# A decoder layer on one core: small TensorE pieces moved to other places of a hand-written order

## The chip, the core and the metric

The kernel runs on one core of a Trainium2 chip. The time is the device time of one execution in microseconds, median of three runs: 906.37 us (906.29 to 906.52). Less is better. All data are float32. TensorE's granted clock in the profile is 0.998 of full speed over the span, so that times of one row can be compared with those of another.

## The reference, cut to what matters

x has 4096 rows (16 batches of 256) of 256 channels. Three stages, each followed by a layer norm:

```python
# 1: four heads of 64 channels against fixed keys k and values v (256 of them)
q = layernorm(x, ln_g, ln_b)
a = x + square(relu(q_h @ k.T)) @ v              # per head h
h = layernorm(x + a)
# 2: 16 heads of 16 channels, 256 queries by 256 keys per batch
attn = gamma * (Q K^T) / 4 + delta * (ap * max(D, 0) + an * min(D, 0))   # D: clipped differences
h = layernorm(h + softmax(attn) @ V @ Wo.T + bo)
# 3: a feed-forward net with one of 8 experts per row
e = argmax(h @ gate_W.T + gate_b)
f = relu(h @ wi.T + wi_b + (h @ A_e.T) @ B_e.T) @ wo.T + wo_b
out = layernorm(h + f)
```

## The kernel before, in words

The order of all work is written out by hand (`tc.manual_schedule()`, L905 on). Engines run side by side, each works through its own queue in that order, and an instruction waits only for semaphores.

**Stage one** takes eight blocks of 512 rows. A block has eight steps m, two channel halves c by four pairs of n. In a step TensorE computes two score tiles in 64x64 tiles (L311, sixteen matmul records in all), ScalarE takes the relu (L319), VectorE the square (L321), and one step later TensorE multiplies with the values (L331, sixteen records). So TensorE's queue reads: scores of step m, values of step m-1, then whatever the list `steps[m]` holds. Such pieces are: turning the normalised rows of the next block into columns (`turn_in`, L292), turning the sums of the last block back (`turn_out`, L354, two halves of four 128x128 transposes) with VectorE's addition (L360, `y`), statistics (L185, L186), the scale (`scaling`, L202 to L240) and the norm of the last block's rows into `hid` (`norm_out`, L245 on ScalarE, then L376 on GpSimd).

PSUM has eight banks. In stage one two of them are the pool psB (`tile_b`), which the pieces use in turn: a third `tile_b` waits until the first has been read. From the end of stage one on (`turns.append(0)`) `tile_b` goes round three banks.

`biases()` (L140 to L172) folds two biases into others, in four parts: spreading bv, its product with Wo (L147), turning `bo` (L154, copied by VectorE into `columns`, L156), and the product with Wq (L161, subtracted by VectorE, L169). The parts stood at steps 2 to 5 of block 1.

During the last block the first pieces of stage two are made: `turned` (L421, rows of batch 0 into columns), `keys` (L460, whose rows SyncE's queue then scatters into kM) and `queries` (L434), at steps 4, 5 and 6. The first block starts by turning its rows (L292), with ScalarE's and VectorE's evictions to `xnT` (L296, L301), after 30 idle transposes (L910).

**Stage two** is a loop over 64 groups n, four heads of one batch each. Group n: scores (`logits`, L612, in 32-row tiles, into four banks that ScalarE has filled with the positive part of the bias, `positive`, L603), attention product of group n-2 (`attend`, L668, 32-column tiles), row maxima on VectorE (L627, which also adds the negative part that GpSimd prepared, `negative`, L591), turns of the score tiles of group n-1 (`turned`, L652, two tiles, then later two more) with the exponential on ScalarE (`exps`, L659), and the subtraction of the maxima (L642, half on GpSimd and half on VectorE). Between the two pairs of turns stands a large piece (queries L434, keys L460, values L482 or the output product L564 of another batch), if there is one; in group 5 there was none. `keep` copies the attention sums out (L681), the values are copied by L490.

**The feed-forward net** of six blocks is spread over groups 15 to 62, eight groups (parts 0 to 7) for each: rows normalised in part 7 of the block before (`rows`, four L245 on ScalarE), turned in part 0 (`turn`, L752, L755), gates in part 1 (`gates`, L767, 64-column tiles, then ScalarE's copy `gT`), routing and the inner products (L838, L850) in parts 2 and 3, the outer product (L868) in parts 4 to 7. Blocks six and seven of the net follow the loop.

The last stage-one block's sums (`rest`, block 7) were turned in group 0 into `y`, measured in groups 16 to 19 and normalised into `hid` in groups 27, 28, 29 and 35 (`LATE`). Block 6 was finished within stage one.

## Time and profile before

| | us |
|---|---|
| median of three runs | 906.37 |
| the profiled execution's own time | 906.51 |
| its span | 904.72 |
| stage one, 0 to 257: TensorE / VectorE / ScalarE / GpSimd busy | 253.49 / 215.56 / 184.64 / 60.97 |
| groups 0 to 14, 257 to 347 | 86.85 / 81.40 / 73.74 / 81.94 |
| groups with the net, 347 to 830 | 481.98 / 377.74 / 302.96 / 244.48 |
| end, 830 to 904.7 | 69.35 / 32.48 / 10.69 / 2.77 |

The 1.79 us between the span and the profiled execution's time lie around the span. A line of the timeline reads: start, duration, engine and source line, operation, out<-in, active rows and columns of TensorE's array, shape, number of records, and in brackets the idle time before it with what ended it. Matmuls are pipelined: one starts before the one ahead of it has ended, so the time that a run of them takes is read from its start to the next start. PE is TensorE, PEld its weight loads, DVE VectorE, ACT ScalarE, POOL GpSimd.

### The profile page before, as it was taken

How to read it: one execution, taken by the hardware profiler on the slowest of the kernel's cores; microseconds unless marked ns; L12 is line 12 of the kernel's file. 1: busy time of each engine (PE TensorE's matmuls, PEld its weight loads, DVE VectorE, ACT ScalarE, POOL GpSimd, SP SyncE). 2: the span in 40 equal slices, each digit the busy share in tenths (PEclk: the TensorE clock that was granted, in tenths of full speed). 3: DMA queues.
4: the chain of work that ended last, by engine and by line, in shares of the span. 5: the costliest groups of instructions: out<-in, count | busy, mean ns of one | idle time of the engine just before them, and what ended most of it. 6: DMA issues, size and time to landing. Idle time of an engine off the chain costs nothing.

```text
span 904.7 us, 19055 instructions
## 1 busy us (share of the span) xinstructions
PE 891.7 (99%) x6940; PEld 548.0 (61%) x6940; DVE 707.2 (78%) x1980; ACT 572.0 (63%) x953; POOL 390.2 (43%) x381
## 2 busy tenths in 40 slices
PE   8999999999999999999999999999999999999997
PEld 4333333333356776578658757865875786587555
DVE  5888898989878998878777887877788788678444
ACT  5767787778688878466556846655674575566111
POOL 1102312231469997534634653573465347344010
PEclk9999999999999999999999999999999999999999
DMA  5411011100001222010111102011110201111101
GB/s 139 147 36 36 31 39 39 65 2 1 4 10 50 71 72 57 13 42 18 39 43 41 50 14 66 17 39 42 41 51 12 68 18 39 41 28 43 24 0 47
DMA packets 44190, 37.01 MB, mean 41 GB/s; under 512 B 14912, under 2 KB 40000, under 8 KB 44096
## 3 DMA queue, kind: packets, MB, share of 16 engines
q1 hardware_dynamic: 43520, 35.52, 14.1%
q8 instruction: 55, 0.90, 0.4%
q14 instruction: 39, 0.32, 0.1%
q10 hardware_dynamic: 576, 0.26, 0.1%
HBM read 21.07 MB, written 6.03 MB: 30 GB/s over the span
## 4 chain that ended last, share of the span: by engine, by line
PE 59%; DVE 1%; ACT 1%; issue 0%; DVEq 0%; ACTq 0%
PE ps_l L838 12%; PE ps_b L652 10%; PE ps_b L868 7%; PE ps_l L612 5%; PE ps_v L668 5%; PE ps_v L868 5%; PE ps_b L564 3%; PE ps_b L482 2%; PE ps_b L434 2%; PE ps_b L460 2%; PE ps_l L850 2%; PE ps_b L767 1%; PE ps_b L752 1%; PE ps_b L421 1%; PE ps_b L838 0%; PE ps_b L812 0%
## 5 line engine op out<-in xcount | busy, mean ns | idle before, releaser
L591 POOL TENSOR_SCALAR neg<-dneg,aneg,delta 128x512 f32<-128x512 f32 x217 | 187.4, 876 | 207.3 <-PE ps_b L652 129.1
L627 DVE CUSTOM_DVE_ANT_0 neg<-ps_l,neg 128x256 f32<-128x256 f32 x512 | 181.6, 420 | 30.1 <-PE ps_l L612 25.6
L603 ACT ACTIVATE ps_l<-dpos,apos_d 128x512 f32<-128x512 f32 x256 | 173.4, 687 | 40.8 <-DVE mx L627 37.5
L321 DVE TENSOR_TENSOR pr<-r 128x1024 f32<-128x1024 f32 x128 | 155.4, 1254 | 31.3 <-ACT r L319 31.0
L659 ACT ACTIVATE pT<-ps_b 128x512 f32<-128x512 f32 x256 | 142.7, 590 | 56.6 <-PE ps_b L652 54.5
L319 ACT ACTIVATE r<-ps_a 128x1024 f32<-128x1024 f32 x128 | 126.5, 1022 | 57.4 <-PE ps_a L311 31.8
L652 PE MATMUL ps_b<-ident,neg 128*128 128x128 f32 x1024 | 139.1, 278 | 2.8 <-ACT pT L659 2.6
L652 PEld LDWEIGHTS ps_b<-ident,neg 128*128 128x128 f32 x1024 | 113.0, 140 | 38.8 <-issue 16.2
L642 POOL TENSOR_TENSOR neg<-neg,mx 128x1024 f32<-128x1024 f32 x65 | 123.8, 1906 | 21.2 <-DVE mx L627 20.2
L331 PE MATMUL ps_v<-pr,vv 64*64 64x512 f32 x1024 | 123.5, 593 | 0.3
L311 PE MATMUL ps_a<-xnT,kT 64*64 64x512 f32 x1024 | 122.2, 592 | 0.7 <-ACT xnT L296 0.4
L838 PE MATMUL ps_l<-xt,wi 128*128 128x512 f32 x248 | 111.5, 595 | 0.0
L642 DVE TENSOR_TENSOR neg<-neg,mx 128x1024 f32<-128x1024 f32 x63 | 92.3, 1465 | 0.3
L346 POOL TENSOR_TENSOR xt<-xt,half 128x512 f32<-128x512 f32 x15 | 23.8, 1585 | 138.4 <-ACT half L345 138.4
L331 PEld LDWEIGHTS ps_v<-pr,vv 64*64 64x64 f32 x1024 | 38.1, 132 | 70.7 <-issue 43.2
L311 PEld LDWEIGHTS ps_a<-xnT,kT 64*64 64x64 f32 x1024 | 37.6, 133 | 67.0 <-issue 55.5
L612 PE MATMUL ps_l<-kM,qT 32*128 32x256 f32 x1024 | 74.8, 401 | 0.4 <-ACT ps_l L603 0.4
L838 PEld LDWEIGHTS ps_l<-xt,wi 128*128 128x128 f32 x248 | 45.3, 190 | 49.0 <-issue 44.6
L868 PE MATMUL ps_b<-wof,hT 128*128 128x256 f32 x304 | 68.4, 380 | 0.0
L668 PE MATMUL ps_v<-pT,vaug 128*32 128x256 f32 x1024 | 67.5, 384 | 0.8 <-ACT pT L659 0.8
L861 DVE TENSOR_SCALAR hT<-ps_l,wib 128x512 f32<-128x512 f32 x43 | 29.8, 746 | 44.0 <-PE ps_l L850 44.0
L868 PEld LDWEIGHTS ps_b<-wof,hT 128*128 128x128 f32 x304 | 57.5, 190 | 9.2 <-issue 1.5
(119 smaller groups left out, 1055.7 us busy)
## 6 DMA issues: line engine op xcount, KB each, us to landing
cT<-in_ctxT SPq DMA_DIRECT2D x16, 256.0 KB
kM<-keys SPq DMA_DIRECT2D x128, 32.0 KB
v<-raw SPq DMA_DIRECT2D x128, 32.0 KB
invs<-rows SPq DMA_DIRECT2D x128, 32.0 KB
x<-in_x SPq DMA_DIRECT2D x7, 512.0 KB
out<-x SPq DMA_DIRECT2D x7, 512.0 KB
frow<-in_frac SPq DMA_DIRECT2D x16, 128.0 KB
wi<-in_wiT SPq DMA_DIRECT2D x1, 1024.0 KB
```

The costliest lines, as they stand in the source:

```text
L311: nc.tensor.matmul(sc[64 * k : 64 * k + 64, h, :], lhsT=kT[64 * h : 64 * h + 64, q, hf * P + 64 * k : hf * P + 64 * k + 64], rhs=self.xnT[ ...
L319: nc.scalar.activation(r, sc, AF.Relu)
L321: nc.vector.tensor_tensor(pr, r, r, ALU.mult)
L331: nc.tensor.matmul(self.acc[k][64 * h : 64 * h + 64, :], lhsT=vv[64 * k : 64 * k + 64, hf, 64 * q : 64 * q + 64], rhs=pr[64 * k : 64 * k + ...
L591: nc.gpsimd.tensor_scalar(self.neg[:, g], self.batch.dneg, aneg[:, h : h + 1], delta, ALU.mult, ALU.mult,)
L603: nc.scalar.activation(banks[g], self.batch.dpos.rearrange("p j k -> p (j k)"), AF.Copy, scale=apos_d[:, h : h + 1],)
L627: nc.vector.tensor_tensor_reduce(out=self.t[:, g, j, :], in0=banks[g][:, j * S : (j + 1) * S], in1=self.neg[:, g, j, :], scale=1.0, scalar ...
L642: eng.tensor_tensor(rows, rows, top.to_broadcast([P, 4, S]), ALU.subtract)
L652: nc.tensor.transpose(ps[:, k * S + j * P : k * S + (j + 1) * P], self.t[:, g, j, k * P : (k + 1) * P], ident,)
L659: nc.scalar.activation(self.pT[:, g, :], self.ps[g], AF.Exp)
L838: nc.tensor.matmul(self.banks[g], lhsT=wi[:, c, f * P : (f + 1) * P], rhs=self.xT[:, c, :], start=(c == 0), stop=False,)
L868: nc.tensor.matmul(ps[:, 0:C], lhsT=self.hT[f][:, j * P : (j + 1) * P], rhs=wof[:, f, :], start=(f == 0), stop=(f == FC - 1),)
```

## The change

Eight edits, none of which adds or removes a matmul:

- The first block's rows are turned by a new `turn_first`: the first channel half goes into two PSUM tiles, ScalarE evicts 256 columns from one and VectorE 256 from the other; the second half goes through a bank of the pool psV.
- The last two parts of `biases()` move from steps 4 and 5 of block 1 to step 1 of blocks 2 and 3, directly ahead of that step's two half turns.
- Block 6 isn't finished within stage one: its sums are turned in group 5 as the large piece (`turn_both`), written into `hid` instead of `y`.
- Blocks 6 and 7 are measured in groups 16 to 21, 27 and 28, scaled together in group 29 and normalised in groups 35 to 37 and 43 (block 6) and 44, 45, 51, 52 (block 7), in place.
- `turned` and `keys` of batch 0 stand together at step 4 of the last block.
- `queries` of batch 0 stands at its step 7, ahead of the last values, and VectorE evicts it instead of ScalarE.
- `gates` stands directly behind `attend` in part 1, instead of behind the large piece; ScalarE's copy of it stands ahead of the first exponential.
- The rows of net block 0 are normalised by GpSimd behind its share of the subtraction in group 14, instead of by ScalarE ahead of the last two exponentials.

```diff
+            def turn_first(self):
+
+                for c in range(CC):
+                    halves = [tile_b(), tile_b()] if c == 0 else [tile_v()] * 2
+                    for j in range(4):
+                        nc.tensor.transpose(
+                            halves[j // 2][:, j * P : (j + 1) * P],
+                            self.xn[:, j, c * P : (c + 1) * P],
+                            ident,
+                        )
+                    if c == 0:
+                        nc.scalar.activation(
+                            self.xnT[:, c, 0:256], halves[0][:, 0:256], AF.Identity,
+                            bias=ln_b[:, c : c + 1], scale=ln_g[:, c : c + 1],
+                        )
+                    part = slice(256 if c == 0 else 0, 512)
+                    nc.vector.tensor_scalar(
+                        self.xnT[:, c, part], halves[1][:, part], ln_g[:, c : c + 1],
+                        ln_b[:, c : c + 1], ALU.mult, ALU.add,
+                    )
...
             def turn_out(self, jj):
-                if jj == 0:
+                if self.tb >= NB - 2:
+                    self.y = hid[:, 4 * self.tb : 4 * self.tb + 4, :]
+                elif jj == 0:
                     self.y = px.tile([P, 4, C], FP, tag="y", bufs=1, name="y")
...
+            def turn_both(self):
+                first, second = self.turn_out(0), self.turn_out(1)
+                next(first)
+                yield
+                next(first, None)
+                [*second]
+                yield
...
                 self.x2 = tile_x()
+                rs, nm = self.by
                 for j in range(4):
+                    if self.tb == 0:
+                        nc.gpsimd.tensor_scalar(
+                            self.x2[:, j, :], hid[:, j, :], rs[:, j : j + 1], nm[:, j : j + 1],
+                            ALU.mult, ALU.add,
+                        )
+                        continue
                     scaled(self.x2[:, j, :], hid[:, 4 * self.tb + j, :], self.by, j)
...
-                ps = tile_b()
+                ps = self.gps = tile_b()
...
+            def keep_gates(self):
                 self.gT = small.tile([P, 256], FP, tag="spread", bufs=1, name="gT")
-                nc.scalar.copy(self.gT, ps[:, 0:256])
+                nc.scalar.copy(self.gT, self.gps[:, 0:256])
...
-        rows_in[0].turn_in(0)
-        rows_in[0].turn_in(1)
+        rows_in[0].turn_first()
...
-        early = [first.turned(), first.keys(), first.queries(), first.vals()]
+        early = [first.turned(), first.keys(), first.queries(True), first.vals()]
...
-            if tb > 0:
+            if 0 < tb < NB - 1:
...
-                for m in range(4):
-                    steps[m + 2].append(lambda: next(output))
+                for m in range(2, 4):
+                    steps[m].append(lambda: next(output))
+            if tb in (2, 3):
+                steps[1].insert(0, lambda: next(output))
...
-                for m, piece in enumerate(early[:3], 4):
-                    steps[m] += [lambda p=piece: step(p), lambda p=piece: step(p)]
+                for m, together in ((4, early[:2]), (7, early[2:3])):
+                    steps[m] += [lambda p=piece: step(p) for piece in together * 2]
...
-        LATE = 27, 28, 29, 35
+        LATE = 44, 45, 51, 52, 35, 36, 37, 43
...
+        rest_mv = const.tile([P, 8, 2], FP, name="mv_rest")
+        measured = 16, 17, 18, 19, 20, 21, 27, 28
...
+            if n == 5:
+                large_piece = rows_in[NB - 2].turn_both()
...
                 older.attend()
+            if ff and part == 1 and n < N:
+                ff.gates()
...
-            if n == 20:
-                near_rest = near_root(rest.mv, 4)
+            if n == 29:
+                near_rest = near_root(rest_mv, 8)
...
                     nxt.positive(1)
+                if ff and part == 1 and n < N:
+                    ff.keep_gates()
                 if last:
                     last.turned(0)
...
-                if prep:
+                if prep and prep.tb:
                     prep.rows()
...
-            if ff and part == 1 and n < N:
-                ff.gates()
...
                 divided.divide()
+            if prep and prep.tb == 0:
+                prep.rows()
...
-            if 16 <= n < 20:
-                row_stats(rest.y[:, n - 16, :], rest.mv[:, n - 16, :])
+            if n in measured:
+                j = measured.index(n)
+                row_stats(hid[:, 4 * (NB - 1 - j // 4) + j % 4, :], rest_mv[:, j, :])
             if n in LATE:
                 j = LATE.index(n)
-                rest.norm_out(by[NB], j, j, nc.gpsimd)
+                rows_in[NB - 1 - j // 4].norm_out(by[NB], j, j % 4, nc.gpsimd)
```

More of the change, by code (lines that the diff above doesn't have):

```diff
@@ L932, in tile_decoder_layer @@
             mv = small.tile([P, 8, 2], FP, tag="mv8", bufs=2, name="mv8")
-            if tb in (0, NB - 1):
+            if tb == 0:
                 nc.vector.memset(mv, 0.0)
-            if tb > 0:
+            if 0 < tb < NB - 1:
                 last = rows_in[tb - 1]
@@ L941, in tile_decoder_layer @@
                 last.mv = mv[:, 4:8]
-                if tb + 1 < NB:
-                    for j in range(2, 4):
-                        steps[7].append(
-                            lambda j=j, tb=tb: last.norm_out(by[tb], 4 + j, j, nc.gpsimd)
-                        )
-                else:
-                    steps[4].append(lambda tb=tb, mv=mv: scale(tb, mv))
-                    for j in range(4):
-                        steps[5 + j // 2].append(
-                            lambda j=j, tb=tb: last.norm_out(by[tb], 4 + j, j, nc.gpsimd)
-                        )
+                for j in range(2, 4):
+                    steps[7].append(
+                        lambda j=j, tb=tb: last.norm_out(by[tb], 4 + j, j, nc.gpsimd)
+                    )
             if tb > 1:
@@ L1022, in tile_decoder_layer @@
         FUSED, FIRST = NB - 2, 15
-        LATE = 27, 28, 29, 35
+        LATE = 44, 45, 51, 52, 35, 36, 37, 43
         six, seven = rows_out[NB - 2 :]
         rest = rows_in[NB - 1]
-        rest.mv = const.tile([P, 4, 2], FP, name="mv_rest")
+        rest_mv = const.tile([P, 8, 2], FP, name="mv_rest")
+        measured = 16, 17, 18, 19, 20, 21, 27, 28
         for n in range(N + 2):
@@ L1049, in tile_decoder_layer @@
                 six.gates()
+                six.keep_gates()
             if n > N:
@@ L1071, in tile_decoder_layer @@
                 prep.scale()
-            if n == 20:
-                by[NB] = scaling_of(rest.mv, newton(rest.mv, near_rest, 4), 4)
+            if n == 29:
+                by[NB] = scaling_of(rest_mv, newton(rest_mv, near_rest, 8), 8)
             if halved:
@@ L1192, in tile_decoder_layer @@
         seven.gates()
+        seven.keep_gates()
         seven.inner(0, range(0, 1))
```

## The prediction, on record before the changed kernel was run

> **What bounds the kernel now.** The page first: TensorE is busy for nearly the whole span.

> ```profile
> ## 1 busy us (share of the span) xinstructions
> PE 891.7 (99%) x6940; PEld 548.0 (61%) x6940; DVE 707.2 (78%) x1980; ACT 572.0 (63%) x953; POOL 390.2 (43%) x381
> ```

> The change removes no matmul, and idle time is 13 us, so only two things can be won: waits, and what TensorE loses between instructions. The latter is read from TensorE's timeline, from start to start, since "busy" overlaps. In stage one a run of 16 records of L311 or L331 takes 1.72 us between its like (15.64 to 17.36). Around an insert:

> ```profile
> 75.42 1.90 PE L331 MATMUL ps_v<-pr,vv 64*64 64x512 f32 x16
> 77.24 1.09 PE L354 MATMUL ps_b<-ident,xt 128*128 128x128 f32 x8
> 78.26 1.95 PE L311 MATMUL ps_a<-xnT,kT 64*64 64x512 f32 x16
> 80.03 1.90 PE L331 MATMUL ps_v<-pr,vv 64*64 64x512 f32 x16
> ```

> L331 lasts 1.82 ahead of the transposes, the L311 behind them 1.77, and eight transposes take 1.02 where eight at 0.109 would be 0.87. So one excursion from 64x64 tiles to 128x128 and back costs 0.11+0.05+0.15, some 0.31 us. The same in the groups, around the gate (L767):

> ```profile
> 359.18 1.89 PE L434 MATMUL ps_b<-xT,wq 128*128 128x256 f32 x8
> 361.01 1.08 PE L767 MATMUL ps_b<-xt,gw 128*64 128x256 f32 x8
> 362.02 1.09 PE L652 MATMUL ps_b<-ident,neg 128*128 128x128 f32 x8
> 363.04 1.15 PE L612 MATMUL ps_l<-kM,qT 32*128 32x256 f32 x16
> ```

> L434 takes 1.83 ahead of the gate, where a product of its shape takes 1.73 (L460, 343.84 to 345.57); L652 behind it 1.02, where 0.97 is usual (505.93 to 506.90). Third, the waits: the longest single one is at the first feed-forward block, where ScalarE normalises four rows (L245) ahead of two exponentials that the attention product L668 needs:

> ```profile
> 347.04 2.07 ACT L245 ACTIVATE x<-hid,nm,rs 128x256 f32<-128x256 f32 x4
> 349.01 1.06 ACT L659 ACTIVATE pT<-ps_b 128x512 f32<-128x512 f32 x2
> ```

> ```profile
> 348.25 0.63 PE L668 MATMUL ps_v<-pT,vaug 128*32 128x256 f32 x4
> 349.65 1.53 PE L668 MATMUL ps_v<-pT,vaug 128*32 128x256 f32 x12 [0.77 <-ACT pT L659]
> ```

> From 348.25 to 351.11 is 2.86 against 1.00 undisturbed: 1.86 us lost.

> **The terms.** Each is a change of the span, with its bounds behind it.

> *Start: -0.31 (-0.4 to 0).* ScalarE's 128x512 eviction (L296) runs 9.03 to 9.81 and L311 starts at 9.87. Now it is shared: VectorE's half starts at 9.03 and by the row of a 128x256 read from PSUM (L470, 0.47) ends at 9.50; ScalarE's half (L450's form, 0.57) starts earlier, at some 8.8. L311 starts at 9.56. The next wait (12.10, on ScalarE's r, which was idle before it) moves along. VectorE's second column block lands at 10.3 as before, and is needed only at step 4.

> *Biases next to turns: +2.74 (-0.6 to +3.3).* Gone from block 1: L154 with its excursion, 0.37+0.11+0.05=0.53, and L161, 1.09+0.11+0.05=1.25. Adjacent to the turns the products alone would cost 0.28 and 1.00: a gain of 0.5. But stage one's psB has two buffers, and now three tiles are asked for in a row: product, first half of the turn, second half. The third waits until VectorE has read the first. In the changed program the fifth of the eight transposes of both turns does wait for VectorE, and no transposition behind the first half did before. VectorE's queue there in block 2 (the row behind the squares is where the copy `columns` now goes):

> ```profile
> 76.95 3.00 DVE L321 TENSOR_TENSOR pr<-r 128x1024 f32<-128x1024 f32 x2 [1.56 <-ACT r L319]
> 79.88 1.27 DVE L360 SCALAR_TENSOR_TENSOR y<-x,ps_b 128x512 f32<-128x512 f32 x2
> ```

> So `columns` (0.39) ends at 80.27, TensorE resumes at 80.33 (0.06 as from 9.81 to 9.87), four transposes with the way out take 0.53, and L311 starts at 80.86 instead of 78.26: +2.60. Queued behind the waiting transposes is everything TensorE has. VectorE then does L360 and four statistics and is done with the next squares at 85.4, before L331 wants them (86.1), so the wait of 0.25 at 83.47 (1.97 instead of 1.72) goes: +2.35, less 0.53, is +1.82. In block 3: L161 from 107.33 to 108.33, half a turn to 108.77, VectorE's squares last until 110.05, its two subtractions 0.22, TensorE resumes at 110.33, L311 at 110.86 instead of 108.36: +2.50, less the wait of 0.33 at 113.57 (2.05), less 1.25: +0.92. Lower bound: no wait. Upper: nothing recovered. The rows decide for the wait.

> *Block 6 turned in group 5: -0.90 (-1.3 to -0.4).* Stage one loses L354 with its excursion (1.02+0.11+0.05=1.18), and with VectorE's and ScalarE's normalisation gone the wait at 234.27 (1.86, 0.14). In group 5 there is room: L652's last turn starts at 291.12, 0.51 late, and L612 then breaks off until 292.80. Now two half turns (0.44 each) stand between. The second needs the buffer that the exponential frees at 291.06; the next score transposes one freed at 292.16; the last one VectorE's L360, 0.675 behind `raw` (291.06+0.69), so 292.4. L612 runs from 293.2 with nothing missing, and L668 follows at 294.27 instead of 293.85: +0.42. VectorE's maxima come 0.57 later, and group 6 takes that up, since its VectorE waits for TensorE (0.47 at 293.68). Bounds of the +0.42: 0, and VectorE's whole added 2 x 0.675 less that 0.47, 0.9. The statistics and norms that move to groups 16 to 52 stand in groups where TensorE has 3.45 us of L868; VectorE idles there (1.63 ahead of 577.71).

> *Turn and keys of batch 0 together: -0.36.* One excursion less: 0.10 behind L421 (0.59, against 0.49 ahead of L482), 0.10 ahead of L460, 0.11, 0.05.

> *Queries ahead of the last values: -0.53 (-0.55 to 0).*

> ```profile
> 247.55 1.90 PE L331 MATMUL ps_v<-pr,vv 64*64 64x512 f32 x16
> 249.37 1.99 PE L434 MATMUL ps_b<-xT,wq 128*128 128x256 f32 x8
> 251.30 1.95 PE L311 MATMUL ps_a<-xnT,kT 64*64 64x512 f32 x16
> 253.06 4.16 PE L331 MATMUL ps_v<-pr,vv 64*64 64x512 f32 x32
> 257.15 1.15 PE L612 MATMUL ps_l<-kM,qT 32*128 32x256 f32 x16
> ```

> From 247.55 to L612 it is 9.60. In the new order 1.72+1.72+1.83+1.92+1.77+0.11=9.07: the same excursion, but the last values no longer wait for their squares. VectorE's eviction of the queries (2 x 0.47, queued behind the last square, 4.8 us after L311's start, and the product, 5.5) ends at 6.5; L612 needs it at 7.4. Without that cover, up to 0.5 is lost.

> *Gates behind the values: -0.90 (-1.8 to -0.6).* Six blocks save 0.10 and 0.05, 0.15 each, if going from 32 to 64 columns costs what every change of tiles costs; if it is free, 0.30. I take 0.15: L612 (32x128) takes 1.07 ahead of L668 (128x32) and of L652 alike. The gate's copy on ScalarE now stands ahead of the first exponential; TensorE has two score turns (1.9) before it wants that buffer.

> [...]

> *Rows of block 0 on GpSimd: -1.15 (-1.87 to 0).* Without L245 the exponentials end at 348.2 and L668 isn't late. But VectorE's subtraction (L642) still ends at 349.25, its maxima at 352.0, and the copies that free PSUM follow (L681, L490, to 353.23); TensorE then waits for buffers around its turn L752, and I get L612 at 355.0 instead of 356.18. On GpSimd the rows start when L240 is done (346.85). No row shows this form: L591 has twice the elements at 0.76 to 1.74, so 0.38 each at best, 1.74 at worst; I take 0.4 to 0.5. Rows end near 349, the next three-row work of GpSimd (L591 x4 from 347.42) is 1.2 later, and L642 ends at 354.6, before the turn that needs it (357).

> VectorE's small L202 took 1.45 at 503.47 while GpSimd's L642 ran from 503.01 to 504.90. [...]

> *Late norms: +0.39 (0 to +0.8).* L752 at 512.51 takes 1.34 where 0.95 is usual: one group earlier GpSimd began with a bias addition (L376, 0.73 at 500.07), which pushed its L642 onto VectorE's L202. That came of a norm in group 29. Now groups 37 and 45 have such norms: two such losses for one.

> **Sum.** -0.31+2.74-0.90-0.36-0.53-0.90-1.15+0.39=-1.02. The span of 904.72 becomes 903.70; with the 1.79 around it (906.51 in all) 905.5; against the median of the runs, which is 0.14 lower, 905.4.

> **Rivals.** (1) The two-buffer wait costs nothing, because VectorE gets to `columns` in time: the bias term is -0.5, and the time 902.1. Against it: the squares occupy VectorE for 2.6 us after the turn has begun. (2) The tile change from 32 to 64 columns is free and group 5 hides the turn: -0.9 and -0.42, 904.1. (3) Slower: VectorE, not TensorE, paces groups 5 to 15. It is busy for 81.4 of the 90 us from 257 to 347, TensorE for 86.85. Then group 5 pays all of 1.35 (+0.93), and the time won on L668 is waited for again before L612 (+1.15): 907.5. This decides from the point where VectorE's maxima start without an idle gap before them; at 293.68 they had one of 0.47, at 349.18 none.

> **Chances.** Forecast 0.53 (own range 904.2 to 906.7), rival 1 0.10, rival 2 0.15, rival 3 0.16, else 0.06. The range goes from rival 1 to rival 3: 902.4 to 907.5. A measurement here tells some 0.2%, 1.8 us, from no change. Below 904.56 lie rival 1, most of rival 2 and some of the forecast: 0.30; above 908.18 the tail of rival 3 and the unforeseen: 0.10; between: 0.60.

> **What would show it.** Right: in blocks 2 and 3 the second half of the turn starts 2 us after the first; L434 1.73 in the gate's groups; no gap at L668 in group 15 but waits around L752; L612 of group 0 straight behind L331. Wrong: turns of blocks 2 and 3 without a break, L767 under 1.0, or L752 late for the rows.

## The result, and the profile after

The changed kernel takes 909.54 us (median of five executions, 909.40 to 911.51) beside 906.38 for the kernel before on the same chip: over all executions the ratio is 1.0042, 95% interval 1.0029 to 1.0054. It is slower; the forecast was 905.4 with a range to 907.5. The five executions lie in two groups, three at 909.40 to 909.54 and two at 911.45 and 911.51, where the kernel before has one (906.29 to 906.99); the profiled execution is of the quick group (909.40, span 907.62), and from here on quick ones are compared with quick ones. First come the 2.90 us between the two spans, afterwards the second group (theory C).

The first row of the page, then TensorE's waits (engine, tile and line, what ended the wait: us in all, times, the longest), both of the changed kernel:

```profile
PE 888.9 (98%) x6940; PEld 548.1 (60%) x6940; DVE 715.7 (79%) x1978; ACT 567.0 (62%) x945; POOL 400.7 (44%) x385
```

```profile
PE ps_l L878 <- DVE mx L658: 2.5, 6, 0.9
...
PE ps_b L377 <- DVE columns L156: 2.2, 1, 2.2
...
PE ps_b L377 <- DVE bq L169: 1.4, 1, 1.4
```

TensorE has the same 6940 instructions and is busy for 2.8 us less, in a span 2.9 us longer: it waits more. The second and third row are the waits of the biases term. The first is in no term of the prediction: six waits, one behind each gate group, for VectorE's maxima.

Where the time went is read by laying the two timelines side by side, score run by score run of stage one and group by group of stage two (L612 before, L643 after), and taking the difference of their starts, which are called marks below. Where the difference changes, something was won or lost:

| step | forecast | between the profiles |
|---|---|---|
| start | -0.31 | -0.37, of which -0.19 by the edit |
| biases, blocks 1 to 3 | +2.74 | -1.73 +2.67 -0.26 +2.53 -0.42 = +2.79 |
| end of stage one and group 5 (block 6, turn and keys, queries) | -1.79 | -2.06 |
| rows of block 0, group 15 | -1.15 | -1.31, and -0.12 ahead of it |
| gates, in their own six groups | -0.90 | 6 x -0.15 = -0.90 |
| **the six groups behind the gates** | none | **+1.17 + 5 x 0.62 = +4.29** |
| late norms | +0.39 | -0.38 +0.39 +0.38 = +0.39 |
| group 23 | none | +0.20 |

Their sum is +2.9. One line was not in the forecast's sum: without it the rest would add up to -1.4.

This is that place, in the second gate group, 24, and the group behind it. TensorE's timeline of the changed kernel, from the gates (L805, L767 before) over two score turns (L683) and the queries (L465, L434 before) to the inner product (L878, L838 before):

```profile
437.73 1.08 PE L805 MATMUL ps_b<-xt,gw 128*64 128x256 f32 x8
438.74 1.09 PE L683 MATMUL ps_b<-ident,neg 128*128 128x128 f32 x8
439.67 1.89 PE L465 MATMUL ps_b<-xT,wq 128*128 128x256 f32 x8
...
442.37 1.15 PE L643 MATMUL ps_l<-kM,qT 32*128 32x256 f32 x16
...
444.38 0.38 PE L820 MATMUL ps_b<-ident,gT 128*128 128x128 f32 x2
445.08 1.12 PE L878 MATMUL ps_l<-xt,wi 128*128 128x512 f32 x2 [0.32 <-DVE mx L658]
```

The same stretch of the kernel before, from the gates on:

```profile
440.38 1.08 PE L767 MATMUL ps_b<-xt,gw 128*64 128x256 f32 x8
441.40 1.09 PE L652 MATMUL ps_b<-ident,neg 128*128 128x128 f32 x8
442.42 1.15 PE L612 MATMUL ps_l<-kM,qT 32*128 32x256 f32 x16
...
444.43 0.38 PE L780 MATMUL ps_b<-ident,gT 128*128 128x128 f32 x2
444.65 2.31 PE L838 MATMUL ps_l<-xt,wi 128*128 128x512 f32 x5
```

L820 starts 0.05 earlier than before, the 0.15 of the gates included; then the inner product starts 0.70 behind it instead of 0.22. That is 0.48 of the 0.62; the rest lies between the next records (0.10 to the second one, 0.04 around the transposes behind). What it waits for is one of the four score banks, free when VectorE has read its maxima. So VectorE's timeline, first of the kernel before, then of the changed one:

```profile
440.49 1.00 DVE L445 TENSOR_SCALAR qT<-ps_b,qscale,bq_s 128x256 f32<-128x256 f32 x2 [0.80 <-PE ps_b L434]
...
442.01 1.22 DVE L642 TENSOR_TENSOR neg<-neg,mx 128x1024 f32<-128x1024 f32 x1
443.71 0.42 DVE L627 CUSTOM_DVE_ANT_0 neg<-ps_l,neg 128x256 f32<-128x256 f32 x1 [0.49 <-PE ps_l L612]
```

```profile
441.60 1.00 DVE L476 TENSOR_SCALAR qT<-ps_b,qscale,bq_s 128x256 f32<-128x256 f32 x2 [1.81 <-PE ps_b L465]
...
443.12 1.22 DVE L673 TENSOR_TENSOR neg<-neg,mx 128x1024 f32<-128x1024 f32 x1
444.25 0.42 DVE L658 CUSTOM_DVE_ANT_0 neg<-ps_l,neg 128x256 f32<-128x256 f32 x1
```

In a gate group VectorE evicts the queries (L445, now L476). Before, their product came first and the gates' product (1.02) behind it; VectorE evicted, divided and subtracted while TensorE worked on the gates, and had 0.49 to spare when the next scores came. Now the gates come first and the queries' product ends a gate's length later. VectorE idles for 1.81 us instead of 0.80, in front of a queue that it then can't catch up: the next maxima start without a gap, 0.54 later, and TensorE waits for the bank.

Behind the first gate group the loss is 1.17, because VectorE had nothing to spare there. In group 16 it also measures a late row (L185, L186), ahead of the next maxima. VectorE in the kernel before, then TensorE in the changed one:

```profile
362.63 1.22 DVE L642 TENSOR_TENSOR neg<-neg,mx 128x1024 f32<-128x1024 f32 x1
363.76 0.42 DVE L185 BATCH_NORM_STATS2 st<-y 128x6 f32<-128x256 f32 x1
364.22 0.18 DVE L186 BATCH_NORM_AGGREGATE mv_rest<-st 128x2 f32<-128x6 f32 x1
364.36 0.42 DVE L627 CUSTOM_DVE_ANT_0 neg<-ps_l,neg 128x256 f32<-128x256 f32 x1
```

```profile
363.78 0.38 PE L820 MATMUL ps_b<-ident,gT 128*128 128x128 f32 x2
365.09 3.27 PE L878 MATMUL ps_l<-xt,wi 128*128 128x512 f32 x7 [0.93 <-DVE mx L658]
```

The maxima start 1.32 behind their scores in the kernel before (363.04 to 364.36), without a gap, and 2.48 behind them in the changed one (361.77 to 364.25). The whole delay comes back there.

### The profile page after: what moved, and what is told of

It is laid out like the page before. It is cut to its first block, busy times and chain, and to the rows that moved or that the text cites. A ratio compares the mean times of both kernels' runs of the same rounds, so it can differ in the third digit from the quotient of the medians.

```text
span 907.6 us, 19067 instructions
## 1 busy us (share of the span) xinstructions
PE 888.9 (98%) x6940; PEld 548.1 (60%) x6940; DVE 715.7 (79%) x1978; ACT 567.0 (62%) x945; POOL 400.7 (44%) x385
## 4 chain that ended last, share of the span: by engine, by line
PE 83%; DVE 9%; ACT 4%; issue 2%; POOL 1%; DMA 1%; DVEq 0%; ACTq 0%
PE ps_l L878 12%; PE ps_v L352 11%; PE ps_a L332 11%; PE ps_b L683 10%; PE ps_b L908 7%; PE ps_l L643 6%; PE ps_v L699 6%; PE ps_v L908 4%; PE ps_b L595 3%; PE ps_b L465 3%; PE ps_b L491 2%; DVE neg L658 2%; DVE pr L342 2%; PE ps_l L890 2%; PE ps_b L513 2%
## 5 line engine op out<-in xcount | busy, mean ns | idle before, releaser
L622 POOL TENSOR_SCALAR neg<-dneg,aneg,delta 128x512 f32<-128x512 f32 x217 | 196.5, 918 | 179.8 <-PE ps_b L683 122.7
L683 PE MATMUL ps_b<-ident,neg 128*128 128x128 f32 x1024 | 138.5, 277 | 2.2 <-ACT pT L690 2.0
L683 PEld LDWEIGHTS ps_b<-ident,neg 128*128 128x128 f32 x1024 | 113.7, 141 | 35.7 <-issue 15.3
L878 PE MATMUL ps_l<-xt,wi 128*128 128x512 f32 x248 | 112.0, 598 | 2.5 <-DVE mx L658 2.5
L673 DVE TENSOR_TENSOR neg<-neg,mx 128x1024 f32<-128x1024 f32 x63 | 96.1, 1526 | 0.3
L878 PEld LDWEIGHTS ps_l<-xt,wi 128*128 128x128 f32 x248 | 45.5, 191 | 53.0 <-issue 44.6
L643 PE MATMUL ps_l<-kM,qT 32*128 32x256 f32 x1024 | 74.1, 400 | 0.0
L407 POOL TENSOR_TENSOR hid<-hid,bo 128x256 f32<-128x256 f32 x32 | 29.4, 935 | 88.7 <-ACT hid L245 69.9
```

What stands on the lines that cost most here:

```text
L622: nc.gpsimd.tensor_scalar(self.neg[:, g], self.batch.dneg, aneg[:, h : h + 1], delta, ALU.mult, ALU.mult,)
L643: nc.tensor.matmul(banks[g][:, j * S : (j + 1) * S], lhsT=self.batch.qT[rows, self.o, j * P : (j + 1) * P], rhs=self.batch.kM[rows, self.i ...
L673: eng.tensor_tensor(rows, rows, top.to_broadcast([P, 4, S]), ALU.subtract)
L683: nc.tensor.transpose(ps[:, k * S + j * P : k * S + (j + 1) * P], self.t[:, g, j, k * P : (k + 1) * P], ident,)
L878: nc.tensor.matmul(self.banks[g], lhsT=wi[:, c, f * P : (f + 1) * P], rhs=self.xT[:, c, :], start=(c == 0), stop=False,)
```

## The experiments

**Theory A**: the loss of 4.3 us is this chain; the gates' product in its old place covered VectorE's eviction of the queries, and ahead of them it doesn't. **R1**: it is the gate's copy, which now stands ahead of the first exponential on ScalarE. **R2**: it comes of other edits (rows measured and normalised in other groups). **R3**: a PSUM bank is held longer by the gate. A later **theory C** is on the second group of times.

**x1: gates and copy at their old place.** The rest of the change stays.

```diff
                 older.attend()
-            if ff and part == 1 and n < N:
-                ff.gates()
...
+            if ff and part == 1 and n < N:
+                ff.gates()
+                ff.keep_gates()
             divided = batches[b - 2] if og == 0 and b >= 2 else None
```

> The changed kernel with one edit undone: the gates' product and its copy stand behind the large piece again. Theory A (the gates' product in its old place covered VectorE's eviction of the queries, its subtraction and the maxima that follow; ahead of the queries it delays this chain): the five later losses of 0.62 and the first of 1.17 behind the gate groups go, 4.3 us together, and 0.2 in groups 23 to 24; the six gains of 0.15 go too. 909.5-4.3-0.2+0.9 = 905.9 us, and group 18 starts 1.2 earlier against group 17 than in the changed kernel. Rival R1 (it is the copy gT that now stands ahead of the first exponential on ScalarE): the same time, since the copy goes back as well; this run can't tell them apart. Rival R2 (the losses come from the rows of blocks 6 and 7, which are measured and normalised in other groups): the losses stay, 909.5+0.9 = 910.4.

Measured: nine executions at 907.36 to 907.93, one at 905.87. In the profile the losses behind the gate groups are gone (-1.17, then five times -0.62 or -0.63) and the gates' groups are 0.15 longer each: as A says, and R2 falls. The profile, of one of the nine, also shows why they lie 1.5 to 2.0 above the expected 905.9. TensorE's rows behind the turn of block 2:

```profile
78.82 3.37 PE L332 MATMUL ps_a<-xnT,kT 64*64 64x512 f32 x16
81.95 2.23 PE L352 MATMUL ps_v<-pr,vv 64*64 64x512 f32 x16
84.00 1.90 PE L332 MATMUL ps_a<-xnT,kT 64*64 64x512 f32 x16
```

and the table by stretches there (from:to, then length, busy time of PE, PEld, DVE, ACT and POOL, the granted clock of TensorE, DMA):

```profile
78.00:80.00 2.00, 1.77 (x12) 0.90 (x16) 1.81 (x5) 0.00 (x0) 0.00 (x0) 0.80 0.00 0
80.00:82.00 2.00, 2.00 (x16) 0.58 (x12) 1.07 (x4) 1.02 (x1) 0.00 (x0) 0.50 0.34 63
82.00:84.00 2.00, 2.00 (x20) 0.68 (x16) 1.52 (x2) 1.02 (x1) 0.00 (x0) 0.85 0.56 199
```

A run of sixteen that takes 1.72 to 1.77 takes 3.13. The granted clock is 0.50 from 80 to 82; the means of 0.80 and 0.85 beside it add 0.8 and 0.6 us at one half, 3.4 us in all, which costs the 1.70 us by which this execution falls behind there. In the quick profile of the changed kernel the clock is 1.00 in all these stretches; its middle one:

```profile
80.00:82.00 2.00, 2.00 (x24) 0.77 (x20) 1.63 (x4) 1.87 (x2) 0.00 (x0) 1.00 0.27 74
```

**x2: the kernel before with the gates' move alone.**

```diff
             older.attend()
+            if ff and part == 1 and n < N:
+                ff.gates()
...
+                if ff and part == 1 and n < N:
+                    ff.keep_gates()
                 if last:
                     last.turned(0)
...
-            if ff and part == 1 and n < N:
-                ff.gates()
             divided = batches[b - 2] if og == 0 and b >= 2 else None
```

> The kernel before with only the gates' product moved behind the attention product and its copy ahead of the first exponential. Theory A: each gate group is 0.15 shorter, each group behind it 0.62 to 1.17 longer: 906.4-0.9+4.3 = 909.8 us. R1: the same. R2 (the other edits make the losses): 906.4-0.9 = 905.5.

Measured: 909.57 (909.45 to 910.21) beside 906.34, ratio 1.0038 (1.0024 to 1.0052). The six gate groups give 0.15 each, the groups behind them lose 1.16 and 5 x 0.61. One edit of eight makes +3.3 us by itself in the marks (+3.2 in the times), with no second group of times.

**x3: ScalarE evicts the queries in the gate groups.** The gates stay where the change puts them.

```diff
-                return nxt and nxt.queries(n > 15 and n % 8 == 0), None, []
+                return nxt and nxt.queries(), None, []
```

> The changed kernel, but the queries of the gate groups are evicted by ScalarE (2 x 0.57) instead of VectorE (2 x 0.5). Theory A: VectorE no longer waits for the delayed product of the queries, so subtraction and maxima come some 1.0 us sooner and the losses of 4.3 go; ScalarE's queue gets 1.15 longer in these groups and may hold up the copies of the bias behind it by part of that: 905.2 to 907 us, without the gap of 0.32 ahead of L838 in group 18's successors. R1 (copy gT ahead of the exponentials): ScalarE is later still, 909.5 or up to 6 x 1.15 more. R3 (the wait is for a PSUM bank that the gate now holds longer): unchanged, 909.5.

Measured: four executions at 904.97 to 905.08, six at 906.64 to 907.21. Against the changed kernel the six losses go (-1.08, then -0.62 or -0.63 each), and the gates' 0.15 stays. TensorE in x3, at the same place:

```profile
443.19 0.38 PE L820 MATMUL ps_b<-ident,gT 128*128 128x128 f32 x2
443.40 3.17 PE L878 MATMUL ps_l<-xt,wi 128*128 128x512 f32 x7
```

From L820 to L878 0.21 again, no wait. The gate is held in its bank as long as before and its copy stands where it stood, so R3 and R1 fall; the late product hurts only through VectorE's queue. ScalarE's added 1.0 us in these groups costs nothing that the marks show.

**x7: the gate's copy behind the first exponentials.**

```diff
-                if ff and part == 1 and n < N:
-                    ff.keep_gates()
                 if last:
                     last.turned(0)
                     last.exps(0)
+                if ff and part == 1 and n < N:
+                    ff.keep_gates()
```

> The changed kernel with the gates' product where it is, but its copy gT behind the first two exponentials on ScalarE instead of ahead of them. Theory A: nothing on the path changes, since the queries' product is as late as before: 909.5, or up to 0.5 per gate group more if a later tile then waits for the bank that the gate holds (912.5). R1: the first exponential comes 0.4 sooner and the losses of 4.3 go: 905 to 906.

Measured: 915.09 (914.89 to 915.27); its profile has the half clock in block 2 too. The losses behind the gate groups stay to 0.02 and each gate group is 0.52 or 0.78 longer. R1 falls a second time, and the copy's early place, which the prediction took to be in time, saves 0.5 to 0.8 a group against a place behind the exponentials.

**x6: the queries' product right behind the gates'.**

```diff
             if ff and part == 1 and n < N:
                 ff.gates()
+                step(large_piece)
```

> The changed kernel with the queries' product directly behind the gates', ahead of the first score turns, in the six gate groups (the large piece's product is issued there; VectorE still evicts the queries). Theory A: the queries' product is at least as early as in the kernel before, so the losses of 1.17 and 5 x 0.62 go and the gates' gain of 0.9 stays: 909.5-4.3 = 905.2 us in the quicker executions (1.7 more in the others, by theory C), plus what the score turns lose if they must wait for one of the three banks, which the gate and the queries now hold: 0 to 0.5 a group, so up to 908.2. If what counts is only which engine evicts: the losses stay, 909.5.

Measured: 911.72, and three executions at 913.20 to 913.92. Expected by theory A were 905.2 to 908.2, and some 1.7 more in the upper group; both groups lie higher. Against the changed kernel each gate group is 0.48 to 0.52 longer, and the groups behind stay as long as they were, but for the first, which wins 0.55. TensorE in x6, at the second gate group as above:

```profile
443.10 1.09 PE L683 MATMUL ps_b<-ident,neg 128*128 128x128 f32 x8 [0.22 <-DVE qT L476]
444.12 1.82 PE L643 MATMUL ps_l<-kM,qT 32*128 32x256 f32 x16
...
447.02 2.31 PE L878 MATMUL ps_l<-xt,wi 128*128 128x512 f32 x5
```

From the scores to L878 are 2.90 us; in the kernel before 2.23 (442.42 to 444.65), in the changed one 2.71. But the scores themselves take 1.82 instead of 1.15: their last bank waits for ScalarE, whose exponentials are late because the second turn waited for the queries' bank (0.22). Take the 0.67 off and 2.23 is left, and VectorE has 0.92 to spare ahead of its maxima, so its chain is mended here and a wait for banks has taken its place, with 0.48 more in the gate group. The three banks, not the order alone, decide where the queries may stand.

**Theory C**: when TensorE stands still for the 2.2 us of block 2's turn, its clock falls to 0.50 for 3.4 us in some executions. x4 takes the stalls out of the changed kernel, x10 puts them into the kernel before.

**x4: the biases' products back in block 1.**

```diff
-                for m in range(2, 4):
-                    steps[m].append(lambda: next(output))
-            if tb in (2, 3):
-                steps[1].insert(0, lambda: next(output))
+                for m in range(4):
+                    steps[m + 2].append(lambda: next(output))
```

> The changed kernel with the last two products of the biases back at steps 4 and 5 of block 1. By the prediction's biases term (+2.74) the stalls of 2.2 and 1.4 us in the turns of blocks 2 and 3 go and 1.78 comes back to block 1: 909.5-2.75 = 906.8 us. Theory C (an idle TensorE of 2.2 us in block 2 also makes its clock fall to 0.5 for 3.4 us in some executions, which costs 1.7 us: 411 of x1's profile): without that stall all executions lie together within 0.8 us, none 1.7 above the others. If the slower executions have another cause, they still appear, at 908.5.

(The 411 in this text is a slip; the place is 79 to 83 us of x1's profile.) Measured: ten executions at 906.29 to 906.93, median 906.5, in one group. In the marks the edit is worth 2.80.

**x10: the kernel before with that move alone.** (x4's diff the other way round.)

> The kernel before with only the two products of the biases moved to step 1 of blocks 2 and 3. By the biases term: 906.4+2.75 = 909.1 us. Theory C: in some executions 1.7 more, 910.8, so two groups of times with nothing between them, and the profile of a slow one shows a granted clock of 0.5 for some 3.4 us just behind block 2's turn, none behind block 3's, whose stall is 1.4. If the two groups come of another edit: all within 0.8 us of 909.1.

Measured: 908.60, and four at 910.29 to 910.58; ratio over all five 1.0040 (1.0026 to 1.0054). Its profile is of the upper group: a stall of 2.23 at 76.2, then a mean clock of 0.55 from 79 to 81 and 0.60 from 81 to 83; the stall of 1.41 in block 3 is followed by 1.00.

**x12: x3, with ScalarE reading the first product.** The stall of 2.2 goes, that of 1.4 stays.

```diff
-        nc.vector.tensor_copy(columns.rearrange("p c f -> p (c f)"), ps[:, 0:C])
+        nc.scalar.copy(columns.rearrange("p c f -> p (c f)"), ps[:, 0:C])
```

> x3 with ScalarE reading the first of the two biases' products (columns), so that block 2's stall of 2.2 us goes and block 3's of 1.4 stays. Theory C, with a fall of the clock that needs the longer stall: 905.0-2.2 = 902.8 us, all executions within 0.8 us. If a stall of 1.4 us is enough: some executions at 904.5.

Measured: five executions at 902.85 to 903.36, one group.

**x13: x3, with the products in blocks 4 and 5.**

```diff
-            if tb in (2, 3):
+            if tb in (4, 5):
```

> x3 with the two biases' products in blocks 4 and 5 instead of 2 and 3. Theory C: the stall of 2.2 us is in block 4 and the fall of the clock goes with it: two groups of times again, about 905.0 and 906.7, and in a slow one's profile a clock of 0.5 behind block 4's turn, none in block 2. If something else in block 2 makes the clock fall: a clock of 0.5 near 80 us as before, or one group at 905.0.

Measured: eight executions at 904.92 to 905.62, two at 906.59 and 906.78. Two groups at the expected times, but the upper one is rarer than in x3. The profile is of the lower group: the stalls have moved (waits of 2.3 and 1.4 us, 2.75 and 2.53 in the marks, at blocks 4 and 5) and the clock is 1.00 behind both, so for this kernel the fall of the clock itself is inferred from the times.

For C stands that all kernels with the long stall have the longer times: two groups, their middles 1.4 to 2.1 apart (the changed one, x1, x3, x6, x10, x11, x13), or the upper group alone (x7, with the half clock in its profile and four executions within 0.4). None without it has two groups (the kernel before, x2, x4, x8, x9, x12, some with only four or five executions).

What decides in which executions it happens can be read from the clock that the traces record. In each profile it rises to full 5.8 to 8.6 us into the span, and every later change comes a multiple of 3.413 us after that: in the kernel before up at 7.60, down at 901.89 (262 times), in the changed one up at 5.82, down at 906.94 (264 times), in x1 up at 7.52, down at 79.20 (21 times), up at 82.61. These are the windows of that grid around block 2's stall, first of the changed kernel with its two half turns, then of x1, which fell:

```profile
75.36 0.60 PE L377 MATMUL ps_b<-ident,xt 128*128 128x128 f32 x4
78.19 0.66 PE L377 MATMUL ps_b<-ident,xt 128*128 128x128 f32 x4 [2.23 <-DVE columns L156]
```

```profile
74.09:77.50 3.41, 1.87 (x18) 0.79 (x10) 2.71 (x2) 1.58 (x2) 2.63 (x3) 1.00 0.20 76
77.50:80.91 3.41, 2.72 (x24) 1.24 (x28) 2.93 (x8) 0.98 (x2) 0.00 (x0) 1.00 0.04 11
```

```profile
75.79:79.20 3.41, 1.18 (x10) 0.63 (x12) 3.25 (x5) 0.00 (x0) 0.97 (x1) 1.00 0.00 0
79.20:82.61 3.41, 3.41 (x20) 1.07 (x16) 2.45 (x6) 1.39 (x2) 0.00 (x0) 0.50 0.39 106
```

In x1 the whole stall lies in one window: TensorE is idle for 2.23 of its 3.41 us, and the next window is at half clock. In the changed kernel's quick execution an edge at 77.50 cuts the stall, 1.54 on one side and 0.69 on the other. All fourteen profiles agree: the clock fell behind every window with 2.18 us idle or more (at block 2 in x1, x6, x7, x10 and x11, and at the end of every program, with 2.54 us in the kernel before), and behind none with 1.84 or less (1.75 at block 2 in x3, 1.30 at block 4 in x13, 1.4 at the shorter stall). So in these profiles the place of the stall on the grid decides. No run set the grid on purpose, and no window had between 1.84 and 2.18.

**x11: the changed kernel, rows of block 0 on ScalarE again.**

```diff
-                if prep and prep.tb:
+                if prep:
                     prep.rows()
...
-            if prep and prep.tb == 0:
-                prep.rows()
```

> The changed kernel with the rows of net block 0 normalised by ScalarE ahead of group 14's last exponentials again. By the prediction's rows term (-1.15; the marks of the changed kernel give -1.43 at group 15): L668 of group 15 is late by some 1.9 again, and part of it is won back at the turn: 909.5+1.15 to 909.5+1.43 = 910.7 to 911.0 us in the quicker executions, 1.7 more in the others. If VectorE's subtraction and maxima bound that place (rival 3): no change, 909.5.

Measured: 910.36, and three at 912.22 to 912.51. Group 15 is 1.30 longer in its marks: the edit is a gain of 1.30, and rival 3 falls.

**x8: x3, with ScalarE reading both of the biases' products.** In the changed kernel the copy stands behind 3 us of VectorE's squares, while ScalarE is idle for 4.2 us.

```diff
-        nc.vector.tensor_copy(columns.rearrange("p c f -> p (c f)"), ps[:, 0:C])
+        nc.scalar.copy(columns.rearrange("p c f -> p (c f)"), ps[:, 0:C])
...
-            nc.vector.tensor_tensor(
-                bq[:, o : o + 1], bq[:, o : o + 1], ps[:, o * P : o * P + 1], ALU.subtract
-            )
+            nc.scalar.activation(
+                bq[:, o : o + 1], ps[:, o * P : o * P + 1], AF.Identity,
+                bias=bq[:, o : o + 1], scale=-1.0,
+            )
```

> The changed kernel with two evictions given to ScalarE: the queries of the gate groups (as in x3, which took the 4.3 away) and both readings of the biases' products (the copy of the columns and the subtraction from bq), which stand behind VectorE's squares in the changed kernel while ScalarE is idle for 4.2 us. If the prediction's account of the biases term is right (the third tile waits for the first to be read), the stalls of 2.2 and 1.4 go and the term becomes about -0.5 instead of +2.74, and so does the slower group of executions: 905.0-3.2 = 901.8 us, in one group. If the turn's second half then waits for VectorE's first addition all the same, nothing is won: 905.0. If ScalarE's relus get late by its 0.4 and 0.5: up to 0.5 above 901.8.

Measured: 901.50 (901.30 to 901.57), ratio to the kernel before 0.9946 (0.9932 to 0.9961), one group. The turn of block 2 in x8:

```profile
75.43 1.28 PE L378 MATMUL ps_b<-ident,xt 128*128 128x128 f32 x8
75.63 0.37 ACT L156 COPY columns<-ps_b 128x256 f32<-128x256 f32 x1
...
76.64 1.95 PE L333 MATMUL ps_a<-xnT,kT 64*64 64x512 f32 x16
```

The eight transposes are one run again. Block 2's mark is 2.20 earlier than in x3, block 3's 1.30: the stall was the wait for the first tile's reader, as the prediction had it.

**x9: x8, and late work in other groups.** No norm in groups 37 and 45, no row measured in group 21.

```diff
-        LATE = 44, 45, 51, 52, 35, 36, 37, 43
+        LATE = 44, 44, 51, 52, 35, 36, 36, 43
...
-        measured = 16, 17, 18, 19, 20, 21, 27, 28
+        measured = 16, 17, 18, 19, 20, 26, 27, 28
```

> x8 with the late norms taken out of groups 37 and 45 (two of them in group 36 and two in 44 instead) and one row measured in group 26 instead of 21. By the prediction's late-norms term a norm in such a group (29, 37, 45) costs the turn two groups later 0.38: -0.77; the 0.2 of group 23, if it comes of the row measured in group 21, goes as well: 901.8-0.97 = 900.8 us. If two norms in one group delay that group's successor instead: 901.8 or more.

Measured: 900.59 (900.52 to 900.76), ratio 0.9937 (0.9922 to 0.9952): faster than both. Groups 39 and 47 give 0.36 each, group 23 0.20, and two norms in one group cost nothing. Of TensorE's waits in x9 these head the list:

```profile
PE ps_v L951 <- POOL ident masks.py:199: 2.5, 1, 2.5
PE ps_b L684 <- ACT pT L691: 2.0, 5, 0.4
```

The first is the start; those of 2.5, 2.2 and 1.4 for VectorE are gone.

## Why the prediction was wrong, step by step

- **The step that failed: "Gates behind the values: -0.90 (-1.8 to -0.6)".** It counted only changes of tiles. That part came to -0.90 exactly (0.15 in each group, not the 0.30 that the prediction estimated for a free change from 32 to 64 columns). What it left out is what stands behind the moved product on TensorE: the queries get late by the gate's length, and VectorE with them. The term was +3.3 (x2), against a bound of -0.6. The rows were there to be read: VectorE's 0.80 of waiting for the queries, and its 0.49 to spare ahead of the maxima (none behind the first gate group), less than the 1.02 by which the product moved. The prediction followed the copy on ScalarE and the tile changes, and asked of no engine but ScalarE what it waits for.
- **Biases next to turns**: +2.74 forecast, +2.79 in the profiles, with both stalls by the mechanism named (third tile, two buffers) and the two later waits won back as worked out. Not foreseen: the clock of 0.50 behind the longer stall in some executions, another 1.7; in the profiles it stands where 2.18 us or more of idling lay in one window of 3.41 us. Rival 1 (no wait) falls.
- **Start**: -0.31 forecast. From the end of ScalarE's second row to the first scores it is 1.48 us in the kernel before and x2, and 1.28 to 1.29 in the changed one, x3, x4, x6, x8 and x9: -0.19. In six other profiles, x10 with the old turn among them, it is 1.38 to 1.83: there the idle transposes ended 0.26 to 0.72 behind that row. The rest of the -0.37 is that those rows began at 7.12 instead of 7.30. The first scores start anywhere from 9.37 to 10.06 over the profiles with the new turn, so the term is within what one execution differs from another.
- **End of stage one and group 5**: -1.79 forecast for three terms, -2.06 found. The turn in group 5 was forecast to cost 0.42; the marks from group 4 to 7 move by -0.65 +1.53 -0.98 = -0.10, so it is hidden, as the second half of rival 2 had it; its first half, a free change of tiles, did not come. No experiment undid these edits; the numbers are differences of two profiles.
- **Rows on GpSimd**: -1.15 forecast, -1.30 by x11. Not in the term: VectorE's subtraction in group 15 took 3.06 us (1.22 in the rows above) beside GpSimd's, which ran from 353.26 to 355.15; the marks show no loss from it. **Late norms**: +0.39 twice, and x9, which takes both away, wins 0.72.
- **Group 23**, +0.20: a row measured in group 21, which the prediction put at nothing because VectorE idles in such groups; x9 took it back together with the norms, and the mark of that group alone moved by -0.20.
- The first gate's loss of 1.17 is the same chain: x3 brings back 1.08 of it.

With the gates' term right the sum would have been -1.02 + 4.2 = +3.2, or 909.6, beside 909.54. That it fits so closely is partly luck: the errors of the other terms (-0.27 at the end of stage one, -0.28 at the rows, +0.20 in group 23, the others under 0.1) add up to -0.36.

## What to carry to other kernels

A piece moved ahead in one engine's queue delays all that it passes: ask for each piece passed who evicts it, what stands behind that eviction on its engine, and how much that engine has to spare; here 0.49 to spare against a piece of 1.02 made the maxima start 0.54 later, and TensorE waited. The remedy here was not the order but the engine: give the eviction to the queue that is idle at that moment (x3 and x8 moved the queries' eviction and two small readings to ScalarE and turned +3.2 into -4.8 us). And a wait on TensorE may cost more than itself: behind this one of 2.2 us the clock of 0.50 took another 1.7 in some executions.
